# Layer 1 feed-forward of a perceiver: units of 256 tokens in a written order, rounding on turned tiles, weights rounded during the self attention

## The chip, the cores and the metric

The kernel runs on one core of a Trainium2 chip. The metric is the device time of one execution in microseconds. Before the change it is 3358.65 us, the median of three runs from 3354.17 to 3358.67.

## The reference

A perceiver of four layers works on x, 16 batches of 64 tokens with 256 features, in fp32. Each layer has a cross attention to a context of 1601 rows a batch, a self attention and a feed-forward part; each of the twelve stages adds to x what it computes from the layer norm of x. The change concerns the feed-forward part of layer 1 and touches the self attention before it. Cut to these two:

```python
# L1_attn (linear attention, 16 heads of 16)
qkv = x @ w_qkv.T + b_qkv            # q, k -> elu + 1
kv_cumsum = cumsum(einsum('bhtd,bhte->bhtde', k_prime, v), axis=2)
out = context / (norm[..., None] + EPS)
return out @ w_out.T + b_out

# L1_ffn
def act_quant(x):                    # per token
    scale = 127.0 / jnp.clip(jnp.max(jnp.abs(x), axis=-1, keepdims=True), 1e-05)
    return jnp.clip(jnp.round(x * scale), -128, 127) / scale
def weight_quant(w):                 # per matrix
    scale = 1.0 / jnp.clip(jnp.mean(jnp.abs(w)), 1e-05)
    return jnp.clip(jnp.round(w * scale), -1, 1) / scale
h = act_quant(x) @ weight_quant(w1).T        # 256 -> 1024
h = depthwise_conv1d(h, conv_w, conv_b)      # 3 taps along the 64 tokens of a batch
h = silu(h)
return act_quant(h) @ weight_quant(w2).T     # 1024 -> 256
```

## The kernel before

x and its layer norm xn lie in SBUF as 8 token tiles of 128 tokens by 256 features. `Net.run` calls the twelve stages in order and, before each, asks for the weights of the next one (`load`), so that w1 and w2 of L1_ffn arrive while L1_attn runs. Whenever a stage finishes a tile of x, `ready` starts its layer norm: statistics on VectorE (lines 300 to 304), a power on GpSimd (305), and the normalisation on VectorE (312), which is emitted together with the next finished tile. The order of instructions on each engine is set by a scheduler, except where `self.fixed` is on: then each instruction that goes through `pinned` keeps the order in which it is written. Each engine executes its own list in order and waits on semaphores for the others.

L1_attn first projects q and k into turned tiles of 512 tokens: ScalarE makes `e` and `z` (1235, 1236), VectorE `qT` (1238). `pair_values` then makes V (1012). After that come 8 token tiles, one after the other: scores S on TensorE, the causal mask `A` on VectorE (1266), `acc` on TensorE, the reciprocal `rec` (1187) and `aT` (1191) on VectorE, `py` on TensorE, and x.

L1_ffn runs in phases over all 1024 tokens. `quant_weight` rounds w1 and w2 to -1, 0, 1 times their mean: a reduce (1722), a matmul with ones, three passes on VectorE (1729 to 1731). The constant MAGIC, added and subtracted, rounds to integers. The tokens get a maximum (1764), a scale (`token_scale`) and three passes each (1768 to 1770), and are turned by TensorE. For each half of 512 tokens and each of 8 chunks of 128 hidden channels, two matmuls make a PSUM tile of one bank; VectorE makes the centre tap with the bias (1783) and adds the two outer taps (1784, 1787), and ScalarE applies SiLU (1790). Then every hidden tile is turned, only to take the maximum per token (1798); the scale of each token is broadcast over the partitions by a matmul with a diagonal (`dg`, 1811, and `sB`), three VectorE passes round the hidden values in place (1818 to 1820), and per token tile eight matmuls with w2 end in x (1825). This stage is not in a fixed order. The helpers record TensorE's work under line 196 (matmul) and line 200 (turn); a matmul of fp32 shows as two records.

Of the kernel before, what the change touches and what calls it, by code (L numbers as in the profile page):

```python
# [44 lines left out]
def _constants():  # L45
# [21 lines left out]
    put("par", ((p[:, None] // 16) % 2) == np.arange(2)[None, :])  # L67
    put("half", (p[:, None] // S) == np.arange(2)[None, :])
    put("iota8", np.broadcast_to(np.arange(8), (P, 8)))
    put("pow", np.broadcast_to(np.array([-0.5, 0.5]), (P, 2)))  # L70
    put("cadd", np.where(same & (p[None, :] <= p[:, None]), 0.0, -1.0e30))
    put("own", (p[:, None] // S) == (np.arange(32)[None, :] // 16))
# [102 lines left out]
class Net:  # L175
# [1030 lines left out]
    def L1_attn(self, w):  # L1206
# [6 lines left out]
        with tc.tile_pool(name="l1a", bufs=1) as wk:  # L1213
# [4 lines left out]
            with (  # L1218
# [7 lines left out]
                for h in range(2):  # L1226
                    tok = slice(h * 512, (h + 1) * 512)
                    for c in range(4):
# [10 lines left out]
                        for i in range(2 * (c // 2)):  # L1239
# [473 lines left out]
            )  # L1713


    def quant_weight(self, small, pst, w):

        nc = self.nc
        wf = w.rearrange("p c n -> p (c n)")
        n = wf.shape[1] * P  # L1720
        a = small.tile([P, 1], F32, tag="wa", name="wa")
        nc.vector.tensor_reduce(a, wf, AX.X, ALU.add, apply_absolute_value=True)
        ps = self.psum(pst, [P, 1], "pst")
        self.mm(ps, self.c("ones"), a)
# [4 lines left out]
        nc.vector.tensor_scalar(wf, wf, s, MAGIC, ALU.mult, ALU.add)  # L1729
        nc.vector.tensor_scalar(wf, wf, MAGIC, 1.0, ALU.subtract, ALU.min)  # L1730
        nc.vector.tensor_scalar(wf, wf, -1.0, m, ALU.max, ALU.mult)

    def token_scale(self, small, am, tag):

        nc = self.nc
        s = small.tile([P, NT], F32, tag=f"s{tag}", name=f"s{tag}")
        nc.vector.tensor_scalar(s, am, 1e-5, None, ALU.max)
        nc.vector.reciprocal(s, s)
        nc.vector.tensor_scalar(s, s, 127.0, None, ALU.mult)
        i = small.tile([P, NT], F32, tag=f"i{tag}", name=f"i{tag}")  # L1740
        nc.vector.reciprocal(i, s)
        return s, i

    def load_L1_ffn(self):
        return self.weights("L1_w1T", "L1_w2T")

    def L1_ffn(self, w):
        nc, tc = self.nc, self.tc
        w1, w2 = w
        NH = 8  # L1750
        cw, cb = self.pv("L1_ffn_conv_w"), self.pv("L1_ffn_conv_b")
        with (
            tc.tile_pool(name="l1f", bufs=1) as wk,
            tc.tile_pool(name="l1fs", bufs=2) as sp,
            tc.tile_pool(name="l1fm", bufs=1) as small,
            tc.tile_pool(name="l1fb", bufs=4) as stat,
            tc.tile_pool(name="l1f_t", bufs=4, space=PSUM) as pst,
            tc.tile_pool(name="l1f_o", bufs=2, space=PSUM) as pso,
        ):
            self.quant_weight(small, pst, w1)  # L1760
            self.quant_weight(small, pst, w2)
            xn = self.xn
            am = small.tile([P, NT], F32, tag="am", name="am")
            nc.vector.tensor_reduce(am, xn, AX.X, ALU.max, apply_absolute_value=True)
            s, inv = self.token_scale(small, am, "x")
            for t in range(NT):
                xt = xn[:, t, :]
                nc.vector.tensor_scalar(xt, xt, s[:, t : t + 1], MAGIC, ALU.mult, ALU.add)
                nc.vector.tensor_scalar(xt, xt, MAGIC, 127.0, ALU.subtract, ALU.min)
                nc.vector.tensor_scalar(xt, xt, -128.0, inv[:, t : t + 1], ALU.max, ALU.mult)  # L1770
            xT = wk.tile([P, 2, NTOK], F32, tag="xT", name="xT")
            self.to_T(pst, "pst", xn, xT)
            hT = wk.tile([P, NH, NTOK], F32, tag="hT", name="hT")
            for h in range(2):
                tok = slice(h * 512, (h + 1) * 512)
                for c in range(NH):
                    ps = self.psum(pst, [P, 8, S], "pst")
                    self.project_T(
                        ps.rearrange("p b s -> p (b s)"), w1, xT, slice(c * P, (c + 1) * P), tok
                    )  # L1780
                    o = hT[:, c, tok].rearrange("p (b s) -> p b s", s=S)
                    tap = [cw[:, 3 * c + i : 3 * c + i + 1] for i in range(3)]
                    nc.vector.tensor_scalar(o, ps, tap[1], cb[:, c : c + 1], ALU.mult, ALU.add)
                    nc.vector.scalar_tensor_tensor(
                        o[:, :, 1:], ps[:, :, : S - 1], tap[0], o[:, :, 1:], ALU.mult, ALU.add
                    )
                    nc.vector.scalar_tensor_tensor(
                        o[:, :, : S - 1], ps[:, :, 1:], tap[2], o[:, :, : S - 1], ALU.mult, ALU.add
                    )
                    nc.scalar.activation(hT[:, c, tok], hT[:, c, tok], AF.Silu)  # L1790

            am2 = small.tile([P, NT, 2], F32, tag="am2", name="am2")
            for t in range(NT):
                for g in range(2):
                    ps = self.psum(pst, [P, 512], "pst")
                    for i in range(4):
                        self.tr(ps[:, i * P : (i + 1) * P], hT[:, 4 * g + i, t * P : (t + 1) * P])
                    nc.vector.tensor_reduce(
                        am2[:, t, g : g + 1], ps, AX.X, ALU.max, apply_absolute_value=True
                    )  # L1800
            amh = small.tile([P, NT], F32, tag="amh", name="amh")
            nc.vector.tensor_reduce(amh, am2, AX.X, ALU.max)
            s, inv = self.token_scale(small, amh, "h")

            sB = wk.tile([P, NTOK], F32, tag="sB", name="sB")
            for h in range(2):
                ps = self.psum(pst, [P, 512], "pst")
                for i in range(4):
                    t = 4 * h + i
                    dg = sp.tile([P, P], F32, tag="dg", name="dg")  # L1810
                    nc.vector.tensor_scalar(dg, self.ident, s[:, t : t + 1], None, ALU.mult)
                    self.mm(ps[:, i * P : (i + 1) * P], self.c("ones"), dg)
                self.evac(sB[:, h * 512 : (h + 1) * 512], ps)
            for h in range(2):
                tok = slice(h * 512, (h + 1) * 512)
                for c in range(NH):
                    o = hT[:, c, tok]
                    nc.vector.tensor_tensor(o, o, sB[:, tok], ALU.mult)
                    nc.vector.tensor_scalar(o, o, MAGIC, MAGIC, ALU.add, ALU.subtract)
                    nc.vector.tensor_scalar(o, o, 127.0, -128.0, ALU.min, ALU.max)  # L1820
                for i in range(4):
                    t = 4 * h + i
                    po = self.psum(pso, [P, D], "pso")
                    self.project_N(po, hT, t, w2)
                    nc.vector.scalar_tensor_tensor(
                        self.x[:, t, :], po, inv[:, t : t + 1], self.x[:, t, :], ALU.mult, ALU.add
                    )
                    self.ready(t)


    def diagonals(self, dst, taps):
# [348 lines left out]
    def run(self, out, stages=STAGES):  # L2180
        tc = self.tc
        with (
            tc.tile_pool(name="const", bufs=1) as const,
            tc.tile_pool(name="stat", bufs=3) as self.stat,
            tc.tile_pool(name="dram", bufs=1, space=bass.MemoryType.DRAM) as self.dram,
            tc.tile_pool(name="wst", bufs=2) as self.wpool,
            tc.tile_pool(name="stream", bufs=2) as self.stream,
        ):
            self.load_constants(const)

            held = {}

            def load(n):
                if n is not None and n not in held:
                    f = getattr(self, f"load_{n}", None)
                    held[n] = f() if f else None

            for i, name in enumerate(stages):
                load(name)
                load(stages[i + 1] if i + 1 < len(stages) else None)  # L2200
                getattr(self, name)(held.pop(name))
                self.normalise()
            for t in range(NT):
                self.nc.sync.dma_start(out[t * P : (t + 1) * P, :], self.x[:, t, :])
# [22 lines left out]
```

## Time and profile before

| what | value |
|---|---|
| runs before | 3358.65 us (3354.17 to 3358.67) |
| profiled execution | 3360.36 us, its span 3358.6 us |
| mean granted TensorE clock | 0.947 |
| busy share of the span | TensorE 91%, weight load 67%, VectorE 42%, ScalarE 35%, GpSimd 14% |
| L1_ffn in the span | about 1832 to 1944 us |
| busy from 1834 to 1945 us | TensorE 87.3, VectorE 99.2, ScalarE 14.6 us |

Times in the profile are counted from the start of the span. A group line names the source line, the engine, the operation, the tile written and the tiles read, the shapes, and the number of instructions; then the busy time, the mean duration in ns of one, and the idle time of the engine just ahead of them with what ended it. A window line has the stretch and its length, the busy time of TensorE, of its weight load, of VectorE, ScalarE and GpSimd, each with its number of instructions, then the mean clock granted to TensorE, the DMA share and the GB/s. A chain line has a start, a duration and what ran.

### The profile page before, as it was taken

How to read it: one execution, taken by the hardware profiler on the slowest of the kernel's cores; microseconds unless marked ns; L12 is line 12 of the kernel's file. 1: busy time of each engine (PE TensorE's matmuls, PEld its weight loads, DVE VectorE, ACT ScalarE, POOL GpSimd, SP SyncE). 2: the span in 40 equal slices, each digit the busy share in tenths (PEclk: the TensorE clock that was granted, in tenths of full speed). 3: DMA queues.
4: the chain of work that ended last, by engine and by line, in shares of the span. 5: the costliest groups of instructions: out<-in, count | busy, mean ns of one | idle time of the engine just before them, and what ended most of it. 6: DMA issues, size and time to landing. Idle time of an engine off the chain costs nothing.

```text
span 3358.6 us, 67892 instructions
## 1 busy us (share of the span) xinstructions
PE 3060.2 (91%) x28823; PEld 2263.5 (67%) x28823; DVE 1426.8 (42%) x3654; ACT 1175.9 (35%) x2367; POOL 470.2 (14%) x478
## 2 busy tenths in 40 slices
PE   7999998689899999999996899999978898888797
PEld 4666665479656666666664567777757777777697
DVE  6888885722244444444447922212242100136300
ACT  3555555211133333333330122222212277752111
POOL 2333322223200000000000000000002311101132
PEclk9999999789899999999996899999988899998799
DMA  6342332179411211211266011111117645510397
GB/s 203 109 131 89 130 106 80 42 281 322 131 44 55 79 64 55 79 59 60 79 209 204 1 52 42 57 59 59 40 39 266 196 154 184 196 49 1 140 322 240
DMA packets 178364, 395.14 MB, mean 118 GB/s; under 512 B 11446, under 2 KB 142270, under 8 KB 165214
## 3 DMA queue, kind: packets, MB, share of 16 engines
q1 hardware_dynamic: 165070, 372.91, 32.3%
q0 software_dynamic: 11712, 16.00, 2.4%
q8 instruction: 228, 3.74, 0.5%
q10 hardware_dynamic: 1280, 1.89, 0.2%
q14 instruction: 74, 0.61, 0.1%
HBM read 375.04 MB, written 16.12 MB: 116 GB/s over the span
## 4 chain that ended last, share of the span: by engine, by line
PE 75%; DVE 11%; DMA 6%; issue 5%; POOL 1%; ACT 1%; SPq 0%; POOLq 0%; DVEq 0%; ACTq 0%
PE acc L196 17%; PE pss L196 15%; PE pst L196 14%; PE pst L200 6%; PE psk L196 5%; PE pso L196 5%; DMA l3o<-y,token 4%; PE s L196 4%; PE p L196 4%; PE ps L196 3%; DVE Sx L448 2%; PE psh L196 2%; DVE Sx L471 1%; PE py L196 1%; POOL rs L305 1%
## 5 line engine op out<-in xcount | busy, mean ns | idle before, releaser
L196 PE MATMUL acc<-ctx,st 128*128 128x257 f32 (+1 forms) x1664 | 397.2, 383 | 0.0
L196 PE MATMUL pss<-qk,ctxT 128*128 128x512 f32 (+1 forms) x832 | 388.9, 592 | 0.6 <-DVE qk L620 0.6
L196 PEld LDWEIGHTS acc<-ctx,st 128*128 128x128 f32 (+1 forms) x1664 | 310.2, 190 | 95.1 <-issue 35.4
L636 DVE TENSOR_TENSOR top<-pss,top 128x512 f32<-128x512 f32 x192 | 132.6, 691 | 399.0 <-ACT st L631 398.8
L448 DVE CUSTOM_DVE_ANT_0 Sx<-s,mneg 128x384 f32<-128x384 f32 (+1 forms) x512 | 262.8, 567 | 78.7 <-PE s L196 70.7
L200 PE MATMUL pst<-cst,Sx 128*128 128x128 f32 (+1 forms) x1736 | 257.0, 286 | 33.5 <-DVE Sx L471 13.5
L492 ACT ACTIVATE PT<-pst 128x384 f32<-128x384 f32 x512 | 221.3, 489 | 154.3 <-PE pst L200 153.0
L305 POOL TENSOR_TENSOR rs<-rs,cst 128x1 f32<-128x1 f32 x96 | 57.2, 598 | 1526.9 <-DVE rs L304 1426.2
L200 PEld LDWEIGHTS pst<-cst,Sx 128*128 128x128 f32 (+1 forms) x1736 | 190.4, 143 | 83.7 <-issue 41.5
L919 ACT ACTIVATE Pr<-pss 128x512 f32<-128x512 f32 (+1 forms) x512 | 220.1, 523 | 64.2 <-PE pss L196 62.8
L196 PEld LDWEIGHTS pss<-qk,ctxT 128*128 128x128 f32 (+1 forms) x832 | 154.2, 186 | 120.7 <-issue 102.7
L660 ACT ACTIVATE st<-st 128x512 f32<-128x512 f32 (+1 forms) x208 | 130.7, 630 | 276.0 <-DVE st L659 276.0
L196 PE MATMUL pso<-W,hT 128*128 128x256 f32 x884 | 200.9, 379 | 0.0
L631 ACT COPY st<-pss 128x512 f32<-128x512 f32 (+1 forms) x208 | 121.6, 585 | 223.1 <-PE pss L196 223.1
L196 PE MATMUL pst<-wst,ctxT 128*128 128x256 f32 (+1 forms) x832 | 183.4, 380 | 0.0
L196 PE MATMUL psk<-ctxT,wst 128*128 128x512 f32 (+1 forms) x512 | 181.8, 513 | 0.8 <-ACT qT L781 0.8
L196 PEld LDWEIGHTS pso<-W,hT 128*128 128x128 f32 x884 | 163.2, 190 | 19.7
L196 PEld LDWEIGHTS pst<-wst,ctxT 128*128 128x128 f32 (+1 forms) x832 | 153.5, 186 | 25.9 <-issue 2.7
L196 PE MATMUL s<-ctxT,q 32*128 32x384 f32 (+1 forms) x1024 | 159.6, 573 | 6.2 <-DVE mx L448 4.7
L196 PE MATMUL pss<-q,ctxT 32*128 32x128 f32 (+1 forms) x3328 | 148.2, 296 | 17.7 <-issue 14.6
L821 DVE TENSOR_TENSOR v<-pst,bvec 128x512 f32<-128x512 f32 (+1 forms) x112 | 73.0, 652 | 196.3 <-PE pst L196 196.3
L196 PEld LDWEIGHTS psk<-ctxT,wst 128*128 128x128 f32 x512 | 88.3, 190 | 93.7 <-issue 92.1
(395 smaller groups left out, 4551.5 us busy)
## 6 DMA issues: line engine op xcount, KB each, us to landing
ctxT<-in_ctxT_dram SPq DMA_DIRECT2D x64, 1601.0 KB
W<-in_L_experts_dram SPq DMA_DIRECT2D x61, 1024.0 KB
ctx<-in_ctx_dram SPq DMA_DIRECT2D x32, 1536.0 KB
W<-in_L_experts_dram SPq DMA_DIRECT2D x23, 1536.0 KB
ctx<-in_ctx_ones_dram SPq DMA_DIRECT2D x16, 1632.0 KB
ctx<-in_ctx_one_dram SPq DMA_DIRECT2D x16, 1542.0 KB
W<-in_L_experts_dram SPq DMA_DIRECT2D x23, 768.0 KB
W<-in_L_experts_dram SPq DMA_DIRECT2D x15, 1028.0 KB
```

Of the source, the lines that this page charges most:

```text
L196: self.pinned(self.nc.tensor.matmul(out, lhsT, rhs, start=start, stop=stop))
L200: self.pinned(self.nc.tensor.transpose(out, in_, self.ident[:n, :n]))
L305: nc.gpsimd.tensor_tensor(rs, rs, self.c("pow")[:, 0:1], ALU.pow)
L448: self.pinned(nc.vector.tensor_tensor_reduce(out=Sx[:, j, :n], in0=ps[j][:, :n], in1=st["mneg"][:, o : o + n], op0=ALU.add, op1=ALU.max, s ...
L471: self.pinned(nc.vector.tensor_scalar(Sj[j], Sj[j], m[:, j : j + 1], None, ALU.subtract))
L492: self.pinned(nc.scalar.activation(PT, ps, AF.Exp))
L631: pin(nc.scalar.copy(st[:kn], ps[:kn]))
L636: pin(nc.vector.tensor_tensor(top[b][:kn], ps[:kn], top[b][:kn], ALU.max))
L660: pin(nc.scalar.activation(st, st, AF.Exp, scale=HD**-0.5))
L821: nc.vector.tensor_tensor(o, ps[:kn, :n, :], bv[:kn].to_broadcast([kn, n, D]), ALU.add)
L919: nc.scalar.activation(st["Pr"][:kn, g : g + n, j, :], ps[j][:kn, :n, :], AF.Silu)
```

## The change

The rounding of w1 and w2 moves into L1_attn, after V and ahead of the scores (`quant_weights`). It is now two reduces into one tile, one matmul, and for each matrix one ScalarE activation (scale and MAGIC) and two VectorE passes. The means are kept in `self.wm`; the mean of w1 is multiplied into the conv weights `cw`, that of w2 into the scale of the hidden tokens.

L1_ffn becomes four units of 256 tokens, in a fixed order of 26 steps. Steps 0 to 15 each do `first`: two chunks of 128 channels share one PSUM tile; per chunk ScalarE makes the centre tap and VectorE adds the outer ones. SiLU of the two chunks (`gate`) follows one step later. From step 5 on, odd steps turn a token tile of hidden values into natural layout in PSUM (`natural`), where VectorE takes the maximum, makes the scale from four small operations, and ScalarE scales and rounds the tile on its way to SBUF; the tile before goes through the matmuls with w2 (`second`). Even steps turn the rounded tile back (`back`), and ScalarE subtracts MAGIC. The rounding of x (`quant`) is done per token tile, two tiles a unit, ScalarE for the scale and VectorE for the rest; `turn_x` turns a unit. The broadcast of scales over partitions and the three passes over the hidden values are gone. In the diff, "..." stands for removed lines of the old L1_ffn that are printed above.

```diff
--- before.py
+++ after.py
@@ -67,6 +67,8 @@
     put("par", ((p[:, None] // 16) % 2) == np.arange(2)[None, :])
     put("half", (p[:, None] // S) == np.arange(2)[None, :])
     put("iota8", np.broadcast_to(np.arange(8), (P, 8)))
+    put("magic", np.full((P, 1), MAGIC))
+    put("-magic", np.full((P, 1), -MAGIC))
     put("pow", np.broadcast_to(np.array([-0.5, 0.5]), (P, 2)))
     put("cadd", np.where(same & (p[None, :] <= p[:, None]), 0.0, -1.0e30))
     put("own", (p[:, None] // S) == (np.arange(32)[None, :] // 16))
@@ -1243,6 +1245,8 @@
                                 self.c("par")[:, i : i + 1], None, ALU.mult,
                             ))
                 V = self.pair_values(wk, pst, xnT, wqkv[:, :, 512:768], self.bv(3))
+                if "L1_ffn" in self.held:
+                    self.quant_weights(small, pst, self.held["L1_ffn"])
             with (
                 tc.tile_pool(name="l1at", bufs=2) as sp,
                 tc.tile_pool(name="l1a_s", bufs=1, space=PSUM) as pss,
@@ -1713,119 +1717,179 @@
             )
 
 
-    def quant_weight(self, small, pst, w):
+    def quant_weights(self, small, pp, ws):
 
         nc = self.nc
-        wf = w.rearrange("p c n -> p (c n)")
-        n = wf.shape[1] * P
-        a = small.tile([P, 1], F32, tag="wa", name="wa")
-        nc.vector.tensor_reduce(a, wf, AX.X, ALU.add, apply_absolute_value=True)
-        ps = self.psum(pst, [P, 1], "pst")
+        self.wm = self.stat.tile([P, 2], F32, tag="wm", name="wm", bufs=1)
+        flat = [w.rearrange("p c n -> p (c n)") for w in ws]
+        a = small.tile([P, 2], F32, tag="wa", name="wa", bufs=1)
+        for i, w in enumerate(flat):
+            nc.vector.tensor_reduce(
+                a[:, i : i + 1], w, AX.X, ALU.add, apply_absolute_value=True
+            )
+        ps = self.psum(pp, [P, 2], "pst")
         self.mm(ps, self.c("ones"), a)
-        m = small.tile([P, 1], F32, tag="wm", name="wm")
-        nc.vector.tensor_scalar(m, ps, 1.0 / n, 1e-5, ALU.mult, ALU.max)
-        s = small.tile([P, 1], F32, tag="ws", name="ws")
-        nc.vector.reciprocal(s, m)
-        nc.vector.tensor_scalar(wf, wf, s, MAGIC, ALU.mult, ALU.add)
-        nc.vector.tensor_scalar(wf, wf, MAGIC, 1.0, ALU.subtract, ALU.min)
-        nc.vector.tensor_scalar(wf, wf, -1.0, m, ALU.max, ALU.mult)
-
-    def token_scale(self, small, am, tag):
-
-        nc = self.nc
-        s = small.tile([P, NT], F32, tag=f"s{tag}", name=f"s{tag}")
-        nc.vector.tensor_scalar(s, am, 1e-5, None, ALU.max)
-        nc.vector.reciprocal(s, s)
-        nc.vector.tensor_scalar(s, s, 127.0, None, ALU.mult)
-        i = small.tile([P, NT], F32, tag=f"i{tag}", name=f"i{tag}")
-        nc.vector.reciprocal(i, s)
-        return s, i
+        nc.vector.tensor_scalar(
+            self.wm, ps, 1.0 / (P * flat[0].shape[1]), 1e-5, ALU.mult, ALU.max
+        )
+        r = small.tile([P, 2], F32, tag="wr", name="wr", bufs=1)
+        nc.vector.reciprocal(r, self.wm)
+        for i, w in enumerate(flat):
+            nc.scalar.activation(
+                w, w, AF.Identity, bias=self.c("magic"), scale=r[:, i : i + 1]
+            )
+            nc.vector.tensor_scalar(w, w, MAGIC + 1.0, MAGIC - 1.0, ALU.min, ALU.max)
+            nc.vector.tensor_scalar(w, w, MAGIC, None, ALU.subtract)
 
     def load_L1_ffn(self):
         return self.weights("L1_w1T", "L1_w2T")
 
     def L1_ffn(self, w):
         nc, tc = self.nc, self.tc
         w1, w2 = w
-        NH = 8
...
+        NH, NU, U = 8, 4, 256
+        pin = self.pinned
+        cb = self.pv("L1_ffn_conv_b")
         with (
...
+            tc.tile_pool(name="l1f", bufs=2) as wk,
             tc.tile_pool(name="l1fs", bufs=2) as sp,
...
+            tc.tile_pool(name="l1fm", bufs=4) as small,
+            tc.tile_pool(name="l1f_p", bufs=3, space=PSUM) as pp,
+            tc.tile_pool(name="l1f_n", bufs=2, space=PSUM) as pn,
+            tc.tile_pool(name="l1f_o", bufs=1, space=PSUM) as po,
         ):
...
+            self.fixed = True
+            cw = wk.tile([P, 3 * NH], F32, tag="cw", name="cw", bufs=1)
+            nc.vector.tensor_scalar(
+                cw, self.pv("L1_ffn_conv_w"), self.wm[:, 0:1], None, ALU.mult
+            )
+            def scales(am, tag):
+                s = small.tile([P, 2], F32, tag=f"s{tag}", name=f"s{tag}")
+                pin(nc.vector.tensor_scalar(s[:, 0:1], am, 1e-5, None, ALU.max))
+                pin(nc.vector.reciprocal(s[:, 0:1], s[:, 0:1]))
+                pin(nc.vector.tensor_scalar(s[:, 0:1], s[:, 0:1], 127.0, None, ALU.mult))
+                pin(nc.vector.reciprocal(s[:, 1:2], s[:, 0:1]))
+                return s
+            xq, xT, hT, nat, sc, hb = {}, {}, {}, {}, {}, {}
+            def quant(t):
+                xt = self.xn[:, t, :]
+                am = small.tile([P, 1], F32, tag="am", name="am")
+                pin(nc.vector.tensor_reduce(am, xt, AX.X, ALU.max, apply_absolute_value=True))
+                s = scales(am, "x")
+                pin(nc.scalar.activation(
+                    xt, xt, AF.Identity, bias=self.c("magic"), scale=s[:, 0:1]
+                ))
+                pin(nc.vector.tensor_scalar(
+                    xt, xt, MAGIC, s[:, 1:2], ALU.subtract, ALU.mult
+                ))
+            def turn_x(u):
+                ps = self.psum(pp, [P, 2, U], "ps")
+                for i in range(2):
+                    for kc in range(2):
+                        self.tr(
+                            ps[:, kc, i * P : (i + 1) * P],
+                            self.xn[:, 2 * u + i, kc * P : (kc + 1) * P],
+                        )
+                xT[u] = wk.tile([P, 2, U], F32, tag="xT", name="xT")
+                pin(nc.scalar.copy(xT[u], ps))
+            def first(u, g):
+                if g == 0:
+                    hT[u] = wk.tile([P, NH, U], F32, tag="hT", name="hT")
+                ps = self.psum(pp, [P, 2, U], "ps")
+                for i in range(2):
+                    c = 2 * g + i
+                    self.project_T(ps[:, i, :], w1, xT[u], slice(c * P, (c + 1) * P), slice(None))
+                for i in range(2):
+                    c = 2 * g + i
+                    tap = [cw[:, 3 * c + k : 3 * c + k + 1] for k in range(3)]
+                    o = hT[u][:, c, :].rearrange("p (b s) -> p b s", s=S)
+                    p = ps[:, i, :].rearrange("p (b s) -> p b s", s=S)
+                    pin(nc.scalar.activation(
+                        o, p, AF.Identity, bias=cb[:, c : c + 1], scale=tap[1]
+                    ))
+                    pin(nc.vector.scalar_tensor_tensor(
+                        o[:, :, 1:], p[:, :, : S - 1], tap[0], o[:, :, 1:], ALU.mult, ALU.add
+                    ))
+                    pin(nc.vector.scalar_tensor_tensor(
+                        o[:, :, : S - 1], p[:, :, 1:], tap[2], o[:, :, : S - 1], ALU.mult, ALU.add
+                    ))
+            def gate(u, g):
+                o = hT[u][:, 2 * g : 2 * g + 2, :]
+                pin(nc.scalar.activation(o, o, AF.Silu))
+            def natural(t):
+                u, i = divmod(t, 2)
+                ps = self.psum(pn, [P, NH, P], "nat")
                 for c in range(NH):
...
+                    self.tr(ps[:, c, :], hT[u][:, c, i * P : (i + 1) * P])
+                am = small.tile([P, 1], F32, tag="am", name="am")
+                pin(nc.vector.tensor_reduce(
+                    am, ps.rearrange("p c q -> p (c q)"), AX.X, ALU.max, apply_absolute_value=True
+                ))
+                sc[t] = scales(am, "h")
+                nat[t] = sp.tile([P, NH, P], F32, tag="nat", name="nat")
+                pin(nc.scalar.activation(
+                    nat[t], ps, AF.Identity, bias=self.c("magic"), scale=sc[t][:, 0:1]
+                ))
+            def back(t):
+                ps = self.psum(pn, [P, NH, P], "nat")
                 for c in range(NH):
...
+                    self.tr(ps[:, c, :], nat[t][:, c, :])
+                hb[t] = sp.tile([P, NH, P], F32, tag="hb", name="hb")
+                pin(nc.scalar.activation(hb[t], ps, AF.Identity, bias=self.c("-magic")))
+                pin(nc.vector.tensor_scalar(
+                    sc[t][:, 1:2], sc[t][:, 1:2], self.wm[:, 1:2], None, ALU.mult
+                ))
+            def second(t):
+                ps = self.psum(po, [P, D], "po")
+                for c in range(NH):
+                    self.mm(ps, hb[t][:, c, :], w2[:, c, :], c == 0, c == NH - 1)
+                pin(nc.vector.scalar_tensor_tensor(
+                    self.x[:, t, :], ps, sc[t][:, 1:2], self.x[:, t, :], ALU.mult, ALU.add
+                ))
+                self.ready(t)
+            quant(0)
+            quant(1)
+            turn_x(0)
+            N = 4 * NU
+            for n in range(N + 10):
+                if n < N:
+                    u, g = divmod(n, 4)
+                    first(u, g)
+                    if u + 1 < NU and g < 2:
+                        quant(2 * u + 2 + g)
+                    if u + 1 < NU and g == 3:
+                        turn_x(u + 1)
+                if 0 <= n - 1 < N:
+                    gate(*divmod(n - 1, 4))
+                t, odd = divmod(n - 5, 2)
+                if n >= 5:
+                    if not odd and t < NT:
+                        natural(t)
+                    if odd and t < NT:
+                        back(t)
+                    if not odd and 0 <= t - 1 < NT:
+                        second(t - 1)
+            self.fixed = False
 
 
     def diagonals(self, dst, taps):
@@ -2188,7 +2252,7 @@
         ):
             self.load_constants(const)
 
-            held = {}
+            held = self.held = {}
 
             def load(n):
                 if n is not None and n not in held:
```

More of the change, by code (lines that the diff above doesn't have):

```diff
@@ L1749, in L1_ffn @@
         w1, w2 = w
-        NH = 8
-        cw, cb = self.pv("L1_ffn_conv_w"), self.pv("L1_ffn_conv_b")
+        NH, NU, U = 8, 4, 256
+        pin = self.pinned
+        cb = self.pv("L1_ffn_conv_b")
         with (
-            tc.tile_pool(name="l1f", bufs=1) as wk,
+            tc.tile_pool(name="l1f", bufs=2) as wk,
             tc.tile_pool(name="l1fs", bufs=2) as sp,
[L1755 to L1758, printed above, removed]
-        ):
[L1760 to L1775, printed above, removed]
-                for c in range(NH):
[L1777 to L1815, printed above, removed]
-                for c in range(NH):
[L1817 to L1828, printed above, removed]
```

## The prediction

> **What bounds the kernel now.** I read the page first for the kernel's bound, then the window table for the stretch that the change touches, then the groups and the chain inside that stretch.
>
> ```profile
> span 3358.6 us, 67892 instructions
> PE 3060.2 (91%) x28823; PEld 2263.5 (67%) x28823; DVE 1426.8 (42%) x3654; ACT 1175.9 (35%) x2367; POOL 470.2 (14%) x478
> ```
>
> TensorE is 91% busy over the span, but that is an average over twelve stages. The window table (busy us of each engine, then the clock) shows the stretch of the change:
>
> ```profile
> 1790.00:1834.00 44.00, 28.31 (x444) 20.41 (x443) 32.04 (x55) 0.00 (x0) 3.29 (x6) 0.69 0.55 171
> 1834.00:1857.00 23.00, 8.34 (x23) 4.27 (x24) 20.03 (x47) 0.60 (x2) 1.45 (x1) 0.51 0.15 36
> 1857.00:1892.00 35.00, 31.25 (x81) 13.40 (x80) 34.61 (x52) 11.94 (x18) 0.00 (x0) 0.98 0.00 1
> 1905.00:1942.00 37.00, 34.99 (x148) 28.01 (x148) 31.42 (x88) 0.92 (x2) 6.46 (x7) 0.92 0.00 1
> 1834.00:1945.00 111.00, 87.31 (x314) 55.28 (x315) 99.16 (x215) 14.59 (x23) 8.46 (x9) 0.84 0.06 15
> 1945.00:1990.00 45.00, 44.22 (x181) 28.27 (x180) 7.25 (x13) 13.38 (x19) 0.00 (x0) 1.00 0.12 43
> ```
>
> From 1834 to 1945 VectorE (99 of 111 us) is the fullest engine, ScalarE does 15 us, and TensorE idles while weights and tokens are rounded. After 1945 TensorE is full again, so any shift of the stage's end is a shift of the kernel's end. Next, the groups of this stretch and, last, pieces of the chain:
>
> ```profile
> L1783 DVE TENSOR_SCALAR hT<-pst,pvec 128x512 f32<-128x512 f32 x16 | 12.8, 800 | 0.3 <-PE pst L196 0.3
> L1784 DVE SCALAR_TENSOR_TENSOR hT<-pst,pvec,hT 128x504 f32<-128x504 f32 x16 | 11.7, 732 | 0.1
> L1790 ACT ACTIVATE hT<-hT 128x512 f32<-128x512 f32 x16 | 10.1, 630 | 22.9 <-DVE hT L1787 22.9
> L1729 DVE TENSOR_SCALAR wst<-wst,ws 128x2048 f32<-128x2048 f32 x2 | 2.6, 1282 | 0.0
> L1825 DVE SCALAR_TENSOR_TENSOR x<-pso,ih,x 128x256 f32<-128x256 f32 x8 | 3.7, 479 | 2.5 <-PE pso L196 2.5
> ```
>
> ```profile
> 1774.51 1.15 PE S L196 x32
> 1775.68 1.24 DVE A L1266
> ...
> 1877.86 0.72 DVE hT L1783
> 1878.58 0.65 DVE hT L1787
> 1879.23 0.65 DVE hT L1784
> ...
> 1933.83 7.10 PE pso L196 x32
> ```
>
> A chunk of 128 hidden channels by 512 tokens costs the chain .72 + .65 + .65 = 2.02 us on VectorE alone; ScalarE only waits for it (22.9 us at L1790). The last x of L1_attn is written at 1831.97 in the timeline, the last normalised tile of L1_ffn ends at 1943.93: the stage takes 112.0 us. Those are the two ends between which I add up.
>
> **The change, part by part.** The two orders, engine by engine, differ only in L1_attn, L1_ffn and the first instructions of L2_xattn; SP and POOL issue the same list, so no DMA is moved; two more columns of constants ride in the first load, at nothing. Against before, TensorE gets 87 matmuls more (64 turn the rounded hidden tiles back), ScalarE 58 activations more.
>
> (1) Weights, in L1_attn. Removed from L1_ffn: two reduces of 2.28 us, six passes of 1.22 to 1.28, and the idle TensorE with them: the first turn of x starts at 1849.4, so 17.5 us lie open between the stages. Added in L1_attn: the two reduces stand ahead of the first two qT instructions on VectorE, which wait for the DMAs of w1 and w2. SP issues these at 1738.7 and 1739.1; the queue carries some 350 GB/s then, so 1 MB after the 1.5 MB ahead of it lands near 1746 and the next near 1749 (my estimate). qT starts at 1748.71, after a VectorE idle of 4.4 us that covers one reduce, and TensorE has other projections until 1774: cost 0, and up to 3 us if both land late, since qT, the elu tiles on ScalarE and their ring wait behind. The passes come after V, ahead of A of tile 0: small ops .3, ScalarE on w1 about 2.05 (128x1024 took 1.057, L1135, doubled less the start), ScalarE on w2 beside two VectorE passes on w1 at 1.22, then two on w2. The passes begin 2.4 us after V and need 4.9: A moves from 1775.68 to 1781.6, **+5.9**. Nothing covers this: the chain there is S, A, acc, rec, aT, py in turn, and the loop of 6.9 us a tile does not recover. The clock, .69 here, may give back an us: I take **+5**.
>
> (2) First layer. A chunk is now 256 tokens: ScalarE centre tap, then two dependent VectorE taps. The nearest rows: ScalarE from PSUM with two pointers .56 (L1924), taps .48 (L1850), the second starting .52 after the first. Two chunks share one PSUM tile, one bank. In the built program the ScalarE tap of the second chunk waits for a VectorE semaphore that only the second tap of the first chunk raises. So a chunk costs .56 + .05 + .52 + .48 + .05 = 1.65 us serially, 32 chunks **53 us** against 16 x 2.02 = 32 us before. This is the term that decides.
>
> The Trainium skill, "PSUM — Partial Sum Buffer", section "PSUM bank collisions raise a hardware error", says why: two engines may not touch one bank and partition quadrant at once, readers included, so accesses are to be guarded by bank, not by address. The row that would suggest otherwise is L1924, where two activations of different tiles run back to back in 1.02 us. By the row, ScalarE would run ahead and VectorE would bound: 2 taps at .40 to .52, some 1.0 a chunk, 32 us. By the rule 53. No run here shows the collision, but the semaphore is in the program, so I take the rule.
>
> (3) Around it on the same two in-order engines. `natural`: one reduce over 1024 (1.21, L1131), three small ops at .18 before ScalarE may start, ScalarE 128x1024 about 1.2 (1.114 at L805 with one pointer, two here). The next first tap is queued behind it: 3.0 us in which no chunk advances. `back`: ScalarE 1.1, plus Silu .63, half of it beside taps. Behind the taps VectorE also carries the layer norm of a finished tile, .7 of which is in the way. A pair of steps: 4 x 1.65 + 3.0 + .6 + .5 less .2 = **10.5 us**. TensorE in a pair: 8 matmuls of 128x256 (a record .222 from the 7.10/32 above, two a matmul) 3.55, w2 3.55, 16 transposes 2: 9.1, beneath it at full clock. `quant` of a later tile adds am .41, four smalls and ScalarE .59, pinned: 1.5 in each of six steps.
>
> (4) The stage from last x to last xn:
> - Head 7.4: quant of tiles 0 and 1 is placed around the last x; until the fourth small 1.3, ScalarE .6, subtract .35 with the layer norm in front .3, four turns .7, copy .6, four matmuls at half clock 3.55.
> - Steps 0 to 4: 5 x 3.3, four quants 6, table load 1.28 and gates 2.6, half a pair's other work 1: 27.5.
> - Steps 5 to 15: 5.5 pairs, 58, and two quants 3: 61.
> - Tail, three more `natural` and `back` in series: reduce, smalls, ScalarE, turn, then the next turn 6.2 twice; last one 1.2 + .6 + 1.2 + 1 + 1.1 + w2 3.55 + x .5 + layer norm 2.1, with waits 12.5: 25.
> Sum **121**, +9 against 112. Gone with the old code, and so in this sum, are the scaling and rounding passes L1818 to L1820 (24 us) and the centre tap L1783 (12.8 us) on VectorE; serial handoffs took their place.
>
> The clock: "TensorE: Matmul & The Clock Gate", section "HAM oscillation — how this bites in real kernels", warns of idle gaps over about 3.4 us. The gaps of steps 5 to 15 are shorter, so by this rule they run at full clock. The row of 1790 to 1834, .69 without any such gap, says that load counts too: 28 busy us of 44 at mixed clock. The head, tail and first steps are no fuller. By the rule too the head would be slow, since TensorE waits there, and the tail fast; by the row a tail at half clock would make the last w2 3.5 dearer, and steps 5 to 15 would lose full clock now and then. I take full clock for both, and keep the 3.5 for the range.
>
> Total: +5 in L1_attn, +9 in L1_ffn: **+14** on the profiled 3360.36, that is 3374.4. The median of the runs, 3358.65, is 1.7 lower: **3373**.
>
> **The rivals.**
> A. *Handoffs overlap better (no change).* The step is .9 us shorter, because `natural` and quant lie beside taps: 16 x .9 = 14, and the sum is 3359. For: VectorE is about 70% and ScalarE 55% busy in my pair. Against: each next instruction is written in fixed order behind the one that waits.
> B. *The design works (faster).* ScalarE takes a third of the conv, and TensorE becomes the bound at 9.1 a pair or VectorE (taps 28, reduces 10, smalls 10, rounding 6, x and norms 13: 67 in all). With a pair at 8.2, stage 102, it is even; with head 7, TensorE's 73 and half the tail, 93, minus 19, +5: 3345. For: the window's VectorE fill. Against: the bank's semaphore. It decides from chunks under 1.2 us.
> C. *Late weights, half clock (much slower).* At half clock a pair needs 18 us on TensorE, above 10.5; such a load raises the clock again, so perhaps a quarter of the pairs: 2 x 7.7 = 15, and 3 from late weights: 3391.
> D. *The change doesn't move the weights' rounding off the path as it says* is in my forecast already: it comes back as 5 of its 17.5 us.
>
> **Numbers.** Forecast (3364 to 3384 by its terms: the 53 is good to 5, head and tail to 4, the +5 lies between 0 and 9) .70; C .10; A .11; B .09. A measurement can tell about 0.2%, 6.7 us. Slower: .70 + .10 less what of the forecast ends under +6.7, .03: .77. Same: A and this .03, .13. Faster: B and the edge of A, .10. Range 3354 to 3390: it cuts B and the far end of C. The forecast's own 3364 to 3384 stands inside it.
>
> **What would show it.** Right: ScalarE's first-layer taps wait for VectorE's second tap, some 16 waits over 1 us; pairs of steps 10 to 11 us apart; A of tile 0 near 1781.6; stage 121. Wrong: taps of both chunks back to back on ScalarE; TensorE over 85% busy in steps 5 to 15; a first L2_xattn kT activation before its present 1954.1.

## The result, and the profile after

The changed kernel takes 3375.24 us, the median of five runs (3372.18 to 3383.07), against 3358.67 before, the median of five (3354.17 to 3364.28). The ratio is 1.0042, with a 95% interval of 1.0028 to 1.0057: slower by 0.4%. The profiled execution took 3375.24 us, its span 3373.5 us, 14.9 more than before.

The window table of the kernel after, in the columns of before: the whole L1_ffn, a stretch of steady steps, and the stage behind it.

```profile
1838.00:1962.00 124.00, 92.72 (x429) 74.02 (x430) 68.90 (x193) 53.28 (x80) 4.39 (x8) 0.87 0.06 16
1898.00:1934.00 36.00, 30.22 (x159) 25.15 (x157) 25.55 (x72) 18.20 (x28) 1.65 (x3) 1.00 0.00 0
1962.00:2007.00 45.00, 44.22 (x190) 29.87 (x189) 7.53 (x13) 12.89 (x17) 0.00 (x0) 1.00 0.10 37
```

VectorE fell from 99 to 69 us and ScalarE took 53, yet the stage is longer. From 1898 to 1934 TensorE is busy for 84%, VectorE for 71%, ScalarE for 51%, and none is full. The groups say where the idle time is. The last field of each line is idle time ahead of the group, with what ended it:

```profile
L1818 ACT ACTIVATE hT<-ps,pvec,cw 128x256 f32<-128x256 f32 x32 | 17.9, 560 | 27.8 <-DVE hT L1824 19.5 <-PE ps L198 8.3
L1824 DVE SCALAR_TENSOR_TENSOR hT<-ps,cw,hT 128x252 f32<-128x252 f32 x32 | 15.4, 480 | 1.1
L1821 DVE SCALAR_TENSOR_TENSOR hT<-ps,cw,hT 128x252 f32<-128x252 f32 x32 | 15.3, 479 | 30.1 <-ACT hT L1818 30.0
L1844 ACT ACTIVATE nat<-nat,cst,sh 128x1024 f32<-128x1024 f32 x8 | 9.6, 1204 | 16.3 <-DVE sh L1776 16.3
```

ScalarE waits for VectorE's taps (L1818) while VectorE waits for ScalarE's tap (L1821): two engines that hand one bank to and fro. The list of waits (who waited for whom: us in total, times, longest) shows that it happens once in each of the 16 steps:

```profile
DVE hT L1821 <- ACT hT L1818: 30.0, 26, 5.7
ACT hT L1818 <- DVE hT L1824: 19.5, 16, 1.8
ACT nat L1844 <- DVE sh L1776: 16.3, 8, 2.4
...
```

In the chain of waits one step reads like this; before, these places held a run of VectorE taps only:

```profile
1917.91 0.46 ACT hT L1818
...
1918.40 0.49 DVE hT L1821
...
1918.91 0.49 DVE hT L1824
...
1919.43 0.57 ACT hT L1818
...
1920.03 0.49 DVE hT L1821
...
1920.54 0.48 DVE hT L1824
1921.02 1.14 DVE am L1839
```

In L1_attn the chain now has the weights' passes between V and A:

```profile
1770.91 0.43 DVE V L1014
...
1771.77 2.10 ACT wst L1739
...
1773.89 1.24 DVE wst L1742
...
1775.15 1.23 DVE wst L1743
1776.38 1.14 DVE wst L1742
```

For all kernels I use the same four marks of the timeline: the end of V, the start of A of tile 0, the end of the last x of L1_attn and the end of the last xn of L1_ffn.

| kernel | V to A | A to last x | L1_ffn | ratio to before, 95% |
|---|---|---|---|---|
| before | 1.3 | 56.3 | 112.0 | 1 |
| after | 7.4 | 57.5 | 120.3 | 1.0042 (1.0028 to 1.0057) |
| e1_bank | 7.3 | 57.2 | 108.4 | 1.0004 (0.9995 to 1.0013) |
| e2_order | 7.4 | 58.1 | 108.6 | 1.0007 (0.9998 to 1.0016) |
| e3_weights | 7.4 | 58.1 | 100.6 | 0.9990 (0.9977 to 1.0002) |
| e4_spread | 4.5 | 55.0 | 120.2 | 1.0026 (1.0012 to 1.0041) |
| e5_before_spread | 4.5 | 56.6 | 100.6 | 0.9962 (0.9948 to 0.9977) |
| e6_all | 4.5 | 55.1 | 107.3 | 0.9991 (0.9983 to 1.0000) |
| e7_undo_move | 1.3 | 61.3 | 127.1 | 1.0048 (1.0031 to 1.0066) |
| e8_half_w2 | 7.4 | 57.7 | 117.2 | 1.0041 (1.0027 to 1.0055) |
| e10_centre | 4.5 | 52.9 | 94.9 | 0.9936 (0.9917 to 0.9955) |
| e11_scale_kept | 1.4 | 56.4 | 94.8 | 0.9943 (0.9926 to 0.9961) |

The three columns of times, in us, are from one profiled execution of each kernel; the ratios are from timed runs beside the kernel before on the same chip.

### The profile page after: what moved, and what is told of

It reads as the page before. It is cut to its first block, busy times and chain, and to the rows that moved or that the text cites. A ratio compares the mean times of both kernels' runs of the same rounds, so it can differ in the third digit from the quotient of the medians.

```text
span 3373.5 us, 68184 instructions
## 1 busy us (share of the span) xinstructions
PE 3063.7 (91%) x28933; PEld 2280.5 (68%) x28933; DVE 1406.6 (42%) x3654; ACT 1217.3 (36%) x2426; POOL 466.8 (14%) x478
## 4 chain that ended last, share of the span: by engine, by line
PE 76%; DVE 11%; issue 5%; DMA 4%; ACT 2%; POOL 1%; SPq 0%; POOLq 0%; ACTq 0%; DVEq 0%
PE acc L198 16%; PE pss L198 15%; PE pst L198 14%; PE pst L202 6%; PE pso L198 5%; PE psk L198 5%; PE p L198 4%; PE s L198 4%; PE ps L198 3%; PE psh L198 3%; DMA l3o<-y,token 3%; DVE Sx L450 2%; DVE Sx L473 1%; PE py L198 1%; POOL rs L307 1%
```

## The experiments

**e1_bank: a bank for each chunk.**

```diff
-                ps = self.psum(pp, [P, 2, U], "ps")
+                ps = [self.psum(pp, [P, 2, U], "ps") for i in range(2)]
...
-                    self.project_T(ps[:, i, :], w1, xT[u], slice(c * P, (c + 1) * P), slice(None))
+                    self.project_T(ps[i][:, 0, :], w1, xT[u], slice(c * P, (c + 1) * P), slice(None))
...
-                    p = ps[:, i, :].rearrange("p (b s) -> p b s", s=S)
+                    p = ps[i][:, 0, :].rearrange("p (b s) -> p b s", s=S)
```

The pool stays at three banks, so TensorE can be three chunks ahead in place of six.

> The changed kernel with one PSUM bank for each chunk in place of one for two, so ScalarE's centre tap of the second chunk no longer waits for VectorE's taps of the first. Theory (the shared bank makes ScalarE and VectorE take turns, 1.65 us a chunk): the 16 waits of 1.06 to 1.8 us on L1818 go, a chunk falls towards VectorE's two taps, about 1.05, where nothing else stands between; a pair of steps from 10.4 to about 8.5 us, in all 10 to 18 us less: 3357 to 3365. Rival (the stage is bound by TensorE's load at clock 0.87, 93 busy us of 124, or by VectorE's own work): the waits go but come back as waits for TensorE, under 4 us less: 3371 or more.

L1_ffn falls from 120.3 to 108.4, and the ratio to 1.0004. The wait is gone, as this line of ScalarE's timeline shows (two first-layer taps in one row, back to back), and the window line of steady steps shows what took its place:

```profile
1895.56 1.01 ACT L1818 ACTIVATE hT<-ps,pvec,cw 128x256 f32<-128x256 f32 x2
```

```profile
1895.00:1921.00 26.00, 25.25 (x140) 21.39 (x139) 20.60 (x56) 15.92 (x25) 1.65 (x3) 1.00 0.00 1
```

TensorE is busy for 25.25 of 26 us. The starts of `natural` on ScalarE at 1902.54, 1911.99 and 1921.01 give pairs of steps of 9.5 and 9.0 us, against 10.4 in the changed kernel, not the 8.5 I gave: TensorE's own work of about 9 us a pair is the floor. The turns at the shared bank were the cause of the stage's loss, and TensorE is the next bound. The ratio comes back only to 1, since L1_attn keeps its 7 us.

**e2_order: both ScalarE taps first, in the shared bank.**

```diff
+                parts = []
                 for i in range(2):
...
                     pin(nc.scalar.activation(
                         o, p, AF.Identity, bias=cb[:, c : c + 1], scale=tap[1]
                     ))
+                    parts.append((o, p, tap))
+                for o, p, tap in parts:
                     pin(nc.vector.scalar_tensor_tensor(
                         o[:, :, 1:], p[:, :, : S - 1], tap[0], o[:, :, 1:], ALU.mult, ALU.add
                     ))
+                for o, p, tap in parts:
                     pin(nc.vector.scalar_tensor_tensor(
```

> The changed kernel, bank still shared, but both ScalarE taps of a step written ahead of the four VectorE taps, so that the bank is handed over once in a step and not three times. Theory (the handoffs are the cost): ScalarE 1.02 and VectorE 4 taps at about .4 to .5 with one handoff, 2.8 in place of 3.3 us a step: 16 x .5 = 8 less, 3367. Rival (TensorE or VectorE bound): under 3 less, 3372 or more; a third, that VectorE now starts later in each step and loses what the first tap gave it, 3375.

L1_ffn is 108.6, as good as with two banks, and the 11.7 us saved are more than the 8 that I expected. A bank may be shared if it changes hands once. A step now takes 2.7 us from its first ScalarE tap to the end of its last VectorE tap:

```profile
1920.75 1.02 ACT L1819 ACTIVATE hT<-ps,pvec,cw 128x256 f32<-128x256 f32 x2
```

```profile
1921.80 0.86 DVE L1824 SCALAR_TENSOR_TENSOR hT<-ps,cw,hT 128x252 f32<-128x252 f32 x2 [0.84 <-ACT hT L1819]
1922.59 0.86 DVE L1828 SCALAR_TENSOR_TENSOR hT<-ps,cw,hT 128x252 f32<-128x252 f32 x2
```

In the changed kernel the same kind of step takes 3.2 us (1917.80 to 1921.02), which is the gain that I expected. A step in which VectorE first does the layer norm of a finished tile takes 3.9 there (1913.50 to 1917.42) and 2.7 here (1918.15 to 1920.84): ScalarE's second tap no longer stands behind that norm. This I had left out.

**e3_weights: the weights' rounding alone, in the old L1_ffn.** The new `quant_weights` and its call in L1_attn; in L1_ffn the two means go into `cw` and into the scale of the hidden tokens, as in the change.

```diff
-            self.quant_weight(small, pst, w1)
-            self.quant_weight(small, pst, w2)
+            cw = wk.tile([P, 3 * NH], F32, tag="cw", name="cw", bufs=1)
+            nc.vector.tensor_scalar(
+                cw, self.pv("L1_ffn_conv_w"), self.wm[:, 0:1], None, ALU.mult
+            )
...
             s, inv = self.token_scale(small, amh, "h")
+            nc.vector.tensor_scalar(inv, inv, self.wm[:, 1:2], None, ALU.mult)
```

> The kernel before with one part of the change alone: the weights rounded in L1_attn by the new code, the feed-forward part otherwise as before. Theory (the move costs +6 at A of tile 0, and saves the two reduces and six passes, 12.2 us, and the waits between): L1_ffn 112 to about 98, L1_attn +6: -8, that is 3351. Rival (the idle TensorE of the head stays for the rounding of x, which is all that it waited for): L1_ffn 108, +6: 3361.

L1_ffn loses 11.4 us, and L1_attn takes 7.8 longer. The sum of -3.6, in place of the -8 that I expected, agrees with the ratio of 0.999, whose interval just reaches 1. The move gains little here, if anything, because most of it comes back in L1_attn.

**e4_spread: the passes in the gaps of L1_attn.**

```diff
-            nc.vector.tensor_scalar(w, w, MAGIC + 1.0, MAGIC - 1.0, ALU.min, ALU.max)
-            nc.vector.tensor_scalar(w, w, MAGIC, None, ALU.subtract)
+            for h in range(2):
+                self.passes.append((w[:, 1024 * h : 1024 * h + 1024], MAGIC + 1.0, MAGIC - 1.0, ALU.min, ALU.max))
+            for h in range(2):
+                self.passes.append((w[:, 1024 * h : 1024 * h + 1024], MAGIC, None, ALU.subtract))
+
+    def weight_pass(self):
+        if self.passes:
+            w, *a = self.passes.pop(0)
+            self.pinned(self.nc.vector.tensor_scalar(w, w, *a))
...
                     if n < NT:
                         scores(n)
+                        self.weight_pass()
```

> The changed kernel with the four VectorE passes over the weights cut in eight halves of 1024 columns, one behind each A of the eight tiles of L1_attn. Theory (the loop of 6.9 us a tile is a chain over TensorE and VectorE in turn, in which VectorE idles about 1.1 us between A and x): the halves of .65 us are hidden, A of tile 0 comes 5 us earlier, 3370. Rival (each half delays rec or x by its own length): 8 x .65 = 5 come back, 3375, unchanged.

From V to the last x it takes 59.5 in place of 64.8, so 5.3 came back, the size that I expected, but not by the way that I gave. A of tile 0 comes only 2.8 earlier; the other 2.5 are in the six rounds from the first x to the seventh, which take 37.3 in place of 39.9 although VectorE does more in them. Why they are shorter I did not test. The two ratios, 1.0026 and 1.0042, lean the same way, though their intervals overlap. A starts 4.5 us after V, not 1.3. The chain shows ScalarE in front of it:

```profile
1771.46 4.09 ACT wst L1741 x2
1775.55 0.02 issue
1775.57 1.24 DVE A L1270
```

**e5_before_spread** is e3_weights with the edit of e4_spread.

> The feed-forward part of the kernel before, the weights rounded in L1_attn with the VectorE passes in eight halves behind the eight A. Theory (the move is worth its 11 us in L1_ffn, 112.0 to 100.6 with the weights moved alone, and spreading takes back 5 of the 7 that it costs in L1_attn): about 9 less than before, a ratio of 0.997. Rival (the gain of the weights alone, 0.999, is all there is, since the halves lengthen the loop of this kernel): 0.999.

The ratio is 0.9962, with an interval that ends at 0.9977: faster than before. The old feed-forward part with the weights well placed beats both kernels: 11.4 us off L1_ffn, 3.5 on L1_attn.

**e6_all** has the edits of e1_bank, e2_order and e4_spread together.

> The changed kernel with one bank for each chunk, both ScalarE taps ahead of the VectorE taps, and the passes spread. Theory (with a bank each or with the taps reordered a pair of steps is already held by TensorE at 9.0, so that the two together bring little more; the spreading brings its 5): L1_ffn about 107, L1_attn +2, ratio to before 0.999. Rival (the two add up, 12 and 12 us): L1_ffn 97, ratio 0.996.

L1_ffn is 107.3 and the ratio 0.9991. The two cures of the shared bank do not add up. TensorE is near its bound after either, busy for 25.25 of 26 us in e1_bank and 25.62 of 26 in e2_order (1898 to 1924); here it is 24.07 of 26 (1890 to 1916), and the pairs of 8.6 to 9.7 us are no shorter.

**e7_undo_move: the change without the move of the weights.**

```diff
-                if "L1_ffn" in self.held:
-                    self.quant_weights(small, pst, self.held["L1_ffn"])
...
             self.fixed = True
+            self.quant_weights(small, pp, w)
```

> The changed kernel with the weights rounded by the new code at the head of L1_ffn in place of L1_attn. Theory (the move is a gain of some 11 in L1_ffn that costs 7 in L1_attn): L1_attn back to 57.6 from the end of V to the last x, L1_ffn 120 plus the two reduces 4.6, the small ops and 7 of passes, some of it beside the layer norm: 131; +4 to +5 on the changed kernel, ratio to before 1.006. Rival (the move was the loss): ratio 1.002 or less.

L1_ffn is 6.8 longer than in the changed kernel, and from V to the last x it takes 62.6, not the 57.6 of before. The order of VectorE explains the rest: the two reduces stand ahead of the last x of L1_attn, one ahead of the last `rec` and one ahead of the last `aT`, as its timeline shows:

```profile
1819.49 2.29 DVE L1726 TENSOR_REDUCE wa<-wst 128x1 f32<-128x2048 f32 x1 [0.37 <-PE acc L198]
...
1824.55 2.23 DVE L1726 TENSOR_REDUCE wa<-wst 128x1 f32<-128x2048 f32 x1
1826.70 0.41 DVE L1193 TENSOR_TENSOR aT<-acc,rec 128x256 f32<-128x256 f32 x1
```

The last round, from x to x, takes 11.3 us in place of 6.7; the six rounds before it take 39.8, against 40.1 before. So 4.5 of the rounding lies in L1_attn and 6.8 in L1_ffn, about the 11 that I gave, split otherwise. From V to the last xn this kernel is 4.6 us longer than the changed one in the profiles, as the theory has it; the timed ratios, 1.0048 and 1.0042, overlap and don't separate the two, so that the move is a gain within the new stage rests on the profiles alone.

**e8_half_w2: half of TensorE's work with w2 left out**, every second hidden chunk in `second`.

```diff
-                for c in range(NH):
-                    self.mm(ps, hb[t][:, c, :], w2[:, c, :], c == 0, c == NH - 1)
+                for c in range(0, NH, 2):
+                    self.mm(ps, hb[t][:, c, :], w2[:, c, :], c == 0, c == NH - 2)
```

> The changed kernel with four of the eight matmuls with w2 left out for each token tile, so the sum over the hidden channels is half. Theory (steps 5 to 15 are bound by the turns of ScalarE and VectorE at one bank, TensorE fits beneath): pairs of steps stay at 10.4; only the tail, where w2 stands in the chain three times with 3.7 to 4.4, loses about 5. Rival (TensorE is the bound of the pairs): 1.8 less in each of 8 pairs, 14 and more.

This settles the main question. Over the 36 us of steady steps TensorE does 25.63 us in place of 30.22, and the pairs, by the start of `natural`, stay at 10.44:

```profile
1898.00:1934.00 36.00, 25.63 (x128) 20.60 (x127) 25.37 (x70) 17.57 (x27) 1.65 (x3) 0.94 0.00 0
```

```profile
1913.04 1.20 ACT L1844 ACTIVATE nat<-nat,cst,sh 128x1024 f32<-128x1024 f32 x1 [1.82 <-DVE sh L1776]
1923.48 1.21 ACT L1844 ACTIVATE nat<-nat,cst,sh 128x1024 f32<-128x1024 f32 x1 [2.31 <-DVE sh L1776]
```

Less work on TensorE is worth nothing there. L1_ffn as a whole is 3 us shorter, less than the 5 that I gave for the tail; the ratio, 1.0041, does not show it.

**e10_centre: the shared conv, with a bank for each chunk of 512.** e5_before_spread, and:

```diff
-                    nc.vector.tensor_scalar(o, ps, tap[1], cb[:, c : c + 1], ALU.mult, ALU.add)
+                    nc.scalar.activation(o, ps, AF.Identity, bias=cb[:, c : c + 1], scale=tap[1])
```

> The kernel of before with the weights moved and spread, and one more part of the change: the centre tap of the first layer on ScalarE, but with chunks of 512 tokens that have a bank each. Theory (sharing the conv between ScalarE and VectorE pays where each chunk has its own bank): VectorE falls from 2.02 to about 1.3 us a chunk, 21 us, TensorE becomes the bound with 32 matmuls at .86, 27.5 us, so the first layer goes from 32.7 to about 28 and L1_ffn from 100.6 to 96; ratio to before 0.995. Rival (ScalarE, in order with SiLU behind the taps, makes the two take turns here too: .78 + 1.3 + .63 a chunk partly in series): no gain or a loss, 0.996 or more.

L1_ffn is 94.9, against 100.6 in e5_before_spread, and the ratio 0.9936, the lowest of all: 3335.53 us (3331.10 to 3345.66) beside 3359.44. Its interval overlaps that of e5_before_spread, so the gain by the shared conv itself rests on the profiles, this one and that of e11_scale_kept (94.8). ScalarE waits for TensorE now, and the steps follow every 1.72 us:

```profile
1863.91 0.78 ACT L1805 ACTIVATE hT<-pst,pvec,cw 128x512 f32<-128x512 f32 x1 [0.38 <-PE pst L197]
1864.72 0.74 DVE L1806 SCALAR_TENSOR_TENSOR hT<-pst,cw,hT 128x504 f32<-128x504 f32 x1 [0.19 <-ACT hT L1805]
1865.50 0.74 DVE L1809 SCALAR_TENSOR_TENSOR hT<-pst,cw,hT 128x504 f32<-128x504 f32 x1
1865.63 0.78 ACT L1805 ACTIVATE hT<-pst,pvec,cw 128x512 f32<-128x512 f32 x1 [0.38 <-PE pst L197]
```

The next ScalarE tap starts at 1865.63, while VectorE's last tap of the chunk before runs until 1866.24: they overlap, each in its own bank. All 64 matmul records of the first layer run without a gap in 28.6 us. Part of this run's lead is in L1_attn: 52.9 us from A to the last x, where the others need 55 and more.

**e11_scale_kept** is e10_centre with the tile that A waits for taken from another pool.

```diff
-        r = small.tile([P, 2], F32, tag="wr", name="wr", bufs=1)
+        r = self.stat.tile([P, 2], F32, tag="wr", name="wr", bufs=1)
```

> The kernel of the last run with the weights' scale wr in a pool that outlives the projections of L1_attn. In the runs with spread passes A of tile 0 still came 4.5 us after V in place of 1.3, and the chain put ScalarE's two weight activations of 4.09 ahead of it: A is laid over the memory of wr, so it waits for their reads. Theory (that reuse is the wait): A 1.3 us after V, 3.2 less, ratio to before about 0.9925. Rival (A would wait for S or for the clock anyway, or the first half pass now waits for ScalarE behind it and delays rec): A earlier, last x not, ratio unchanged at 0.9936.

The reuse was the wait: A starts 1.4 us after V. But from V to the last x it takes 57.8, against 57.5, and the ratio of 0.9943 is no better: the six rounds between the first x and the seventh took 36.3 us in e10_centre and 39.0 here, with the same instructions. The windows over 50 us, most of it these rounds, first e10_centre, then this kernel, differ in TensorE's granted clock (the number after the five engines):

```profile
1779.00:1829.00 50.00, 33.20 (x636) 25.00 (x636) 42.66 (x74) 0.16 (x1) 3.85 (x7) 0.74 0.61 202
```

```profile
1776.00:1826.00 50.00, 38.81 (x636) 29.14 (x636) 39.80 (x71) 2.29 (x2) 3.58 (x7) 0.61 0.77 235
```

The two intervals overlap, so no gain was seen; with one profile each, whether the earlier start lowers the clock or the two executions fell differently stays open.

## Why the prediction was right

- *The first layer (53 us, the term that decides).* Right in mechanism, and in size where the steps are steady. ScalarE waits for VectorE's second tap in 16 places, 1.06 us where nothing else is queued and up to 1.8 where a layer norm stands ahead of the taps; two chunks of a step follow each other after 1.62 to 1.63 us (1.65 predicted), or 2.33 with the norm. The four chunks of a pair, with `gate`, `back` and the norm beside them, take 7.5 us (1913.50 to 1921.02), and 7.5 is what the terms for these add up to. e1_bank and e2_order show the turns at the bank as the cause, and e8_half_w2 excludes TensorE. Going by the semaphore in the program, and not by the row of L1924, was the step that gave the sign: by the row, the taps run back to back in 1.02 us, which is what they do in e1_bank (1.01). What the chip would do without the semaphore no run here shows.
- *Pairs of steps, 10.5.* Measured 10.43 (`natural` at 1912.39 and 1922.82).
- *The stage.* Head 7.6 (7.4), steps 0 to 4 23.6 (27.5), steps 5 to 15 64.1 (61), tail 25.0 (25); together 120.3 against 121. The two middle terms were off by 4 and 3 in opposite directions, so the sum is better than its parts, and that much is luck. The written order has three of the six `quant` in steps 0 to 4 and three later, where I put four and two. One costs 2.2 us and not 1.5: the pair with two of them takes 14.9 (`natural` at 1887.06 and 1901.97). Three of these and 5.5 pairs of 10.43 make the 64.1. In steps 0 to 4 I added the gates in series, but ScalarE does them, and then the next step's first tap, while VectorE is at its taps: without a `quant`, step 3 starts 2.6 us after step 2 (1854.99 and 1857.58), not 3.3 and a gate.
- *The clock in the stage.* I took full clock from step 5 on, because TensorE's gaps there would be shorter than 3.4 us. One was 5.2 us long (until 1877.46), and the granted clock from 1872 to 1880 was 0.50; from 1860 to 1920 it was 0.85. It cost little: the pair behind it took 10.85 us in place of 10.43.
- *L1_attn.* A moved by 6.0 (5.9). I then took +5, as I hoped for an us from the clock; measured is +7.2 from V to the last x, so this step was short by 2.2, and the clock went the other way. Of the 1.2 beyond A's own shift, 0.95 lie between A and the first x (10.02 in place of 9.07). There the scores of the second tile take longer for the same 32 records, first before, then after:

```profile
1776.96 1.12 PE S L196 x32
```

```profile
1779.96 1.98 PE S L198 x32
```

The granted clock was 1.00 from 1774 to 1778 before, where this S stands, and 0.50 from 1778 to 1782 after. Another 0.46 is in the last round, where small operations of `quant` stand (7.18 in place of 6.72), and the six rounds between are 0.2 shorter. Why the clock is at half there is open: TensorE idles 7.25 us ahead of this S after the change and 1.34 before, but in e11_scale_kept it takes 1.99 after 1.35 idle.
- *The reduces at nothing.* Right: from the first qT to the end of V it takes 25.7 us before and after, with one reduce done before ScalarE's z is ready and the second qT 1.0 us later.
- *The sum.* +7.2, +8.3, and .9 more until the first kT of L2_xattn: 16.4 in this region, 14 predicted. In the profiled pair the V of L1_attn happens to end 3.0 earlier and the rest takes 1.5 longer, which makes the 14.9 of the spans. The mark I gave for A, 1781.6, was missed for that reason alone (1778.7).
- *The rivals.* B needs chunks under 1.2; e1_bank, which has them, reaches no change and not a gain, because TensorE holds the pairs at 9.0 and 7 us remain in L1_attn. One sign against me came close: TensorE was busy for 77% of the time from 1867 to 1931, but for 84% from 1898 to 1934, where 85% was the mark; only e8_half_w2 settles it. C did not come: w1 was there by 1742.4.

## What to carry to other kernels

When work is shared between two engines, count handoffs before busy time. In this program semaphores make two engines that read different halves of one PSUM bank take turns; a bank for each chunk, or one handoff in a step, was worth 12 us of 120. Work moved under an earlier stage is free only where that stage idles on the same engine: of the 11.4 us that the early weights save in L1_ffn, passes put ahead of the serial chain gave back 7.8 in L1_attn, and passes in the chain's gaps 3.5. And a part of a losing change can win: its shared conv with a bank for each chunk, and its early weights, placed in the gaps, make the kernel with the old stage 0.64% faster (interval 0.45 to 0.83%).

## What the runs showed of the hardware

Six rounds of L1_attn with the same instructions took 36.3 and 39.0 us in two kernels (e10_centre, e11_scale_kept). Over just these rounds the granted clock was 0.78 and 0.63; VectorE was busy for 31.1 and 31.4 us, TensorE for 25.1 and 29.2. The other three kernels with this loop fit in: 37.3 us at 0.73 (e4_spread), 37.6 at 0.68 (e6_all) and 39.2 at 0.59 (e5_before_spread). In this chain, which leaves TensorE idle for about a quarter to a third of the time, a lower clock went with up to 3 us more, as much as some edits here were worth. Single profiles of such a stage do not rank edits below that, and the timed ratios here are good to 3 to 6 us either way.
